# Two halves of a gathered tile's TensorE transposes, issued one step apart

## The chip, the cores and the metric

The kernel runs on one core of one Trainium2 chip. The metric is the device time of one execution in microseconds, of which the median of several runs is given. Lower is better.

The engines are named as in the profile: PE is TensorE (matmuls and transposes) and PEld its weight loads, DVE is VectorE, ACT is ScalarE, POOL is GpSimd, SP is SyncE.

## The reference

The kernel computes two residual blocks on 625 rows of 1024 floats. The first is a relational graph convolution on 20000 edges with two relations. The second, which holds the change, is a mixture of eight experts, each row going to its two best, beside two shared experts:

```python
gates = xf @ rW + rb
topk_vals, topk_idx = jax.lax.top_k(gates, TOP_K)          # 2 of 8
topk_probs = jax.nn.softmax(topk_vals, axis=-1)
...
h = _gelu(jnp.einsum('td,edh->eth', xf, W1) + b1[:, None, :])   # 1024 -> 256
y = jnp.einsum('eth,ehd->etd', h, W2) + b2[:, None, :]          # 256 -> 1024
moe = jnp.einsum('te,etd->td', w, y)
return (shared + moe).reshape(B, L, D)
```

The sizes are D = 1024 and 256 hidden columns; all is float32.

## The kernel before

**The experts on gathered rows.** Each row needs only two of the eight experts. The kernel sorts the (row, expert) pairs into `NJ` = 11 tiles of 128 slots. Seven of them (4 to 10) hold rows of one expert, three (0 to 2) hold two halves of 64 slots with an expert each, and one (3) four quarters of 32 slots. Which expert a part belongs to is known only at run time, so weights are addressed by a register (`w1a[:, bass.ds(e, 1)]`).

A tile's normalized rows are gathered from DRAM (`h2d`) by an indirect DMA that GpSimd issues. They lie there as 128 rows of 1024; the product needs them as eight blocks of 128 x 128 with the 1024 on the partitions. This turning is done in one of two ways, in `fetch`:

- Five tiles (4, 6, 7, 8, 9) are gathered by one DMA of full rows. TensorE turns them with eight transposes (line 1441), four into each of two PSUM banks of the tag `acc`, of which there are five. ScalarE copies the first bank to `xsT` (line 1447), VectorE the second (line 1445).
- Six tiles (5, 0, 1, 2, 10, 3; `by_quarters`) are gathered by four DMAs of a quarter of the columns each (line 1424). One VectorE transpose (line 1429) turns the whole tile.

**The loop.** The tiles go in the order 4, 5, 6, 0, 7, 1, 8, 2, 9, 10, 3. Step `s` of the loop issues three things, each for another tile: `fetch` of tile `s` (gather and turning), `expert_in` of tile `s - 1` and `expert_mid` of tile `s - 2`:

```python
for s in range(NJ + 2):
    if s < NJ:
        fetch(tiles[s])
    if 0 <= s - 1 < NJ:
        expert_in(tiles[s - 1])
    if 0 <= s - 2 < NJ:
        expert_mid(tiles[s - 2])
```

`expert_in` (line 1462) multiplies the turned tile by W1 in eight steps of 128 rows; the first four steps read the first half of `xsT`, the other four the second half. In the trace a step of a whole tile is two matmuls. VectorE copies the 256 columns of the result to `hj` (line 1466). `expert_mid` turns that by two TensorE transposes (line 1474), and ScalarE applies Gelu with the bias (line 1477). ScalarE also makes copies of W1 for the parts of tiles 0 to 3 behind the first (`copy_w1`, line 1456), four instructions in each of six steps.

**What sets the order.** Each engine works through its own queue in order, and in this stage the queues stand in the order in which the program issues. `tc.issue_after` puts an instruction behind another one on its engine: the VectorE transpose of a tile stands behind the last copy of line 1445 (`turned[-1]`), the copies of W1 behind the last ScalarE instruction kept in `acts`.

**Buffers.** The gathered rows `xs` have three buffers (pool `io`), so the gather of a tile waits until the tile three places earlier in the order has been turned: 0 for 4, 7 for 5, 1 for 6, 8 for 0, 2 for 7, 9 for 1, 10 for 8, 3 for 2. `xsT` and `hj` have two buffers each; products use PSUM banks of the tag `mm`, of which there are three.

After the stage the second products (line 1522) follow, then the scatter of their rows, the shared experts' output (line 1577) and the sum.

## Time and profile before

| | |
|---|---|
| median of 3 runs | 288.99 us (287.6 to 293.84) |
| the profiled execution, its own time | 290.18 us |
| its span, first to last instruction | 288.4 us |
| TensorE busy | 277.2 us (96%) |
| VectorE, ScalarE, GpSimd busy | 171.8, 100.2, 65.1 us |
| the chain that ended last, by engine | PE 82%, DVE 12%, issue 3%, ACT 1% |
| matmuls of line 1462 (expert_in) | 40.1 us and 14.7 us (copied W1) |
| transposes of line 1441, one | 0.275 us, 40 of them |
| copy of line 1445, one | 0.692 us, 5 of them |
| VectorE transpose of line 1429, one | 2.05 us, 6 of them |
| gather issue of line 1424, one | 0.949 us, 24 of them |

The profile page is one execution taken by the hardware profiler. Its times count from the first instruction. A line of the timeline gives the start and the length in us, the engine, the line of the kernel, the operation with what it writes and reads, the shape, the number of instructions merged into it (x8), and in brackets the idle time of the engine before it with what ended the wait. Matmuls are pipelined: their starts are recorded, their ends are modelled, so those of neighbours overlap. The stage of the change lies between 158 and 207 us.

### The profile page before, as it was taken

Reading aid. Unit: us, or ns where it says so; the run is one execution under the profiler, and the core shown is the slowest. Engines: PE = TensorE matmul, PEld = TensorE weight load, DVE = VectorE, ACT = ScalarE, POOL = GpSimd, SP = SyncE. Lnnn points to the kernel's source line nnn. Section 1 sums busy time; section 2 is a strip of 40 time slices with the busy share of each in tenths; the row PEclk is TensorE's granted clock in tenths of the full one; section 3 lists DMA queues with packets and bytes.
Section 4 is the critical chain, followed back from the end, with each engine's and each line's share of the span. In section 5 each row is a group of like instructions: output and inputs, shape, how many; then the busy total and the mean of one; then the engine's idle time right before and its main releaser. Section 6 shows DMA issues by size and latency. Waiting matters only on the chain.

```text
span 288.4 us, 4459 instructions
## 1 busy us (share of the span) xinstructions
PE 277.2 (96%) x1531; PEld 186.5 (65%) x1531; DVE 171.8 (60%) x433; ACT 100.2 (35%) x232; POOL 65.1 (23%) x128
## 2 busy tenths in 40 slices
PE   8999999999999999899999988999999999999991
PEld 6877777788888455677777877788543344444460
DVE  6899999999874898657800522446143111159820
ACT  3366328243642422453011414854397111000000
POOL 9910110000000124320151656541022222100000
PEclk9999999999999999999999999999999999999997
DMA  7999960000002999996999344321185545399441
GB/s 230 358 333 368 403 216 28 0 0 2 1 0 74 383 391 426 423 403 206 418 406 400 101 145 130 128 60 53 45 338 231 213 190 220 133 374 376 150 142 43
DMA packets 22107, 61.58 MB, mean 214 GB/s; under 512 B 2490, under 2 KB 8317, under 8 KB 21056
## 3 DMA queue, kind: packets, MB, share of 16 engines
q1 hardware_dynamic: 16106, 44.31, 41.3%
q0 software_dynamic: 5680, 16.58, 16.0%
q10 hardware_dynamic: 294, 0.35, 0.6%
q8 instruction: 14, 0.23, 0.3%
q14 instruction: 13, 0.11, 0.1%
HBM read 43.19 MB, written 18.82 MB: 215 GB/s over the span
## 4 chain that ended last, share of the span: by engine, by line
PE 82%; DVE 12%; issue 3%; ACT 1%; DVEq 0%; ACTq 0%
PE p_pr L944 18%; PE p_yj L1522 13%; PE p_o L1577 12%; PE p_h L1462 11%; PE p_sh L1209 11%; PE p_agg L961 5%; PE scrap L1024 2%; PE p_y L1007 2%; DVE xh L1011 2%; PE cnt L923 2%; DVE xsT L1429 1%; DVE st L776 1%; DVE h L749 1%; PE p_t L841 1%; PE p_gate L1155 1%
## 5 line engine op out<-in xcount | busy, mean ns | idle before, releaser
L944 PE MATMUL p_pr<-wg,nT 128*125 128x286 f32 x240 | 61.7, 408 | 0.5 <-ACT nT L847 0.3
L944 PEld LDWEIGHTS p_pr<-wg,nT 128*125 128x125 f32 x240 | 43.4, 187 | 12.7 <-ACT nT L847 1.4
L1462 PE MATMUL p_h<-w1a,xsT 128*128 (+2 forms) x176 | 40.1, 381 | 1.3 <-DVE xsT L1429 1.1
L1522 PE MATMUL p_yj<-w2a,hjT 128*128 (+2 forms) x88 | 38.6, 594 | 0.0
L1577 PE MATMUL p_o<-sw,shT 128*125 128x512 f32 (+1 forms) x88 | 36.1, 553 | 0.0
L1209 PE MATMUL p_sh<-h2T,sw 128*128 128x313 f32 (+1 forms) x128 | 35.3, 429 | 0.0
L1462 PEld LDWEIGHTS p_h<-w1a,xsT 128*128 128x128 f32 (+2 forms) x176 | 28.7, 168 | 8.1 <-issue 1.1
L1209 PEld LDWEIGHTS p_sh<-h2T,sw 128*128 128x128 f32 x128 | 23.6, 189 | 8.5 <-issue 0.2
L1522 PEld LDWEIGHTS p_yj<-w2a,hjT 128*128 128x128 f32 (+2 forms) x88 | 14.4, 168 | 22.4 <-issue 22.4
L1526 DVE COPY ys<-p_yj 128x512 f32<-128x512 f32 x15 | 10.4, 692 | 28.7 <-PE p_yj L1522 26.6
L1577 PEld LDWEIGHTS p_o<-sw,shT 128*125 128x125 f32 x88 | 16.4, 187 | 16.9 <-issue 16.2
L1424 POOL DMA_INDIRECT xs<-h2d,tok x24 | 22.8, 949 | 19.6 <-PE p_x L1441 7.3
L1018 POOL DMA_DIRECT2D x1d<-xh x10 | 5.9, 588 | 71.0 <-DVE flagf L726 62.0
L1466 DVE COPY hj<-p_h 128x256 f32<-128x256 f32 x11 | 4.6, 415 | 27.5 <-PE p_h L1462 12.5
L1530 POOL DMA_INDIRECT yt<-ys,row x11 | 10.7, 973 | 40.8 <-DVE ys L1526 40.8
L1007 PE MATMUL p_y<-wo_t,eT 128*125 128x512 f32 (+1 forms) x40 | 18.8, 592 | 0.0
L1477 ACT ACTIVATE hjT<-p_hT,vT 128x128 f32<-128x128 f32 (+2 forms) x34 | 8.8, 335 | 25.1 <-remote 11.0
L1553 DVE SCALAR_TENSOR_TENSOR x<-p_o,x 125x512 f32<-125x512 f32 (+1 forms) x11 | 6.9, 639 | 15.6 <-PE p_o L1579 15.6
L961 PE MATMUL p_agg<-P,CT 125*125 125x288 f32 x100 | 15.5, 305 | 0.0
L1462 PE MATMUL p_h<-w1m,xsT 128*64 128x256 f32 (+1 forms) x96 | 14.7, 381 | 0.0
L1522 PE MATMUL p_yj<-w2m,hjT 128*64 128x512 f32 (+1 forms) x48 | 14.1, 595 | 0.0
L899 DVE TENSOR_TENSOR ohs<-ohs,cols 125x1024 f16<-125x1024 f16 (+1 forms) x22 | 13.9, 633 | 0.0
(304 smaller groups left out, 412.0 us busy)
## 6 DMA issues: line engine op xcount, KB each, us to landing
w1a<-in_L_ffn_W_dram SPq DMA_DIRECT2D x8, 1024.0 KB
w2a<-in_L_ffn_W_dram SPq DMA_DIRECT2D x8, 1024.0 KB, 5.0
yt<-zero SPq DMA_DIRECT2D x2, 2560.0 KB
g<-yt SPq DMA_DIRECT2D x10, 512.0 KB, 7.3
sw<-in_L_ffn_sW_dram SPq DMA_DIRECT2D x4, 1024.0 KB, 6.2
x<-x1d SPq DMA_DIRECT2D x5, 500.0 KB
x1d<-xh POOLq DMA_DIRECT2D x5, 448.0 KB
h2d<-h POOLq DMA_DIRECT2D x5, 448.0 KB
```

Source lines behind the costliest of these rows:

```text
L899: last = nc.vector.tensor_tensor(os, os, both(VV_, 128)[1], op=ALU.mult)
L944: nc.tensor.matmul(p[:TP, :F], nT[:, k, m * TP : (m + 1) * TP], wg[:, k, r, :], start=(k == 0), stop=(k == KD - 1))
L961: nc.tensor.matmul(p[:TP, : F + 2], CT[:, m, at : at + TP], P[:, m, r, i], start=(m == 0 and i == 0), stop=(m == NT - 1 and i == 1))
L1007: nc.tensor.matmul(ps[s][:TP, :], eT[:n, k, :], wo_t[:n, k, at], start=(k == 0), stop=False)
L1209: nc.tensor.matmul(p[:, : z - a], sw1[:, i, k, t * 128 : (t + 1) * 128], h2T[:, k, a:z], start=(k == 0), stop=(k == KD - 1))
L1424: nc.gpsimd.indirect_dma_start(out=xs[:, a], out_offset=None, in_=h2d.rearrange("n (b f) -> (n b) f", b=4), in_offset=bass.IndirectOffsetO ...
L1462: nc.tensor.matmul(p[a:b, :H], xsT[j][:, k, a:b], w1m[j, a][:, 0, k, :] if a else w1a[:, bass.ds(e, 1), k, :], start=(k == 0), stop=(k == ...
L1477: done = nc.scalar.activation(hjT[:, j, t, a:b], p[:, t * 128 + a : t * 128 + b], AF.Gelu, bias=bT[:, bass.ds(e, 1), t])
L1522: made = nc.tensor.matmul(p[a:b], hjT[:, j, k, a:b], w2m[j, a, k][:, at] if a else w2a[:, bass.ds(e, 1), k, at], start=(k == 0), stop=(k = ...
L1526: nc.vector.tensor_copy(y[:, at], p)
L1530: sent.append(nc.gpsimd.indirect_dma_start(out=yt, out_offset=bass.IndirectOffsetOnAxis(ap=row[:, j : j + 1], axis=0), in_=y, in_offset=No ...
L1577: nc.tensor.matmul(p[:TP, :n], shT[:, i, k, own], sw2[:, i, k, at], start=(i == 0 and k == 0), stop=False)
```

## The change

The turning by TensorE is moved into a function `turn(j, g)` for one half. `fetch` issues only the first half. The second half is issued at the beginning of the next step, ahead of the next tile's `fetch` and so directly in front of the tile's own `expert_in`. The transposes, the copies, their engines and their buffers are the same; the gathered rows are read for the last time one step later.

```diff
         t_ = xt.tile([128, KD, 128], F32, tag="xsT", name=f"xsT_{j}")
-        for g in range(2):
-            p = ps_acc(f"p_x{g}_{j}")
-            for k in range(4):
-                nc.tensor.transpose(p[:, k * 128 : (k + 1) * 128], xs[:, 4 * g + k :: KD], ident)
-            o = t_[:, 4 * g : 4 * g + 4, :]
-            pv = p.rearrange("p (k n) -> p k n", k=4)
-            if g:
-                turned.append(nc.vector.tensor_copy(o, pv))
-            else:
-                acts.append(nc.scalar.copy(o, pv))
         xsT[j] = t_
+        half_row[j] = xs
+        turn(j, 0)
         copy_w1(j)
+
+    half_row = {}
+
+    def turn(j, g):
+        p = ps_acc(f"p_x{g}_{j}")
+        for k in range(4):
+            nc.tensor.transpose(p[:, k * 128 : (k + 1) * 128], half_row[j][:, 4 * g + k :: KD], ident)
+        o = xsT[j][:, 4 * g : 4 * g + 4, :]
+        pv = p.rearrange("p (k n) -> p k n", k=4)
+        if g:
+            turned.append(nc.vector.tensor_copy(o, pv))
+        else:
+            acts.append(nc.scalar.copy(o, pv))
...
     for s in range(NJ + 2):
+        if 0 < s <= NJ and tiles[s - 1] in half_row:
+            turn(tiles[s - 1], 1)
         if s < NJ:
             fetch(tiles[s])
```

## The prediction

> Names: T(j,0) and T(j,1) are the two halves of the transposes of tile j by TensorE, A(j) and V(j) their copies out of PSUM by ScalarE and VectorE, S(j) the VectorE transpose of a tile gathered by quarters, P(j) the eight products of expert_in, hj(j) the copy of its result, M(j) the two transposes of expert_mid. The tiles go 4, 5, 6, 0, 7, 1, 8, 2, 9, 10, 3; TensorE turns 4, 6, 7, 8 and 9.

> **What bounds the kernel.** First the page: the shares and the chain.

> ```profile
> span 288.4 us, 4459 instructions
> PE 277.2 (96%) x1531; PEld 186.5 (65%) x1531; DVE 171.8 (60%) x433; ACT 100.2 (35%) x232; POOL 65.1 (23%) x128
> PE 82%; DVE 12%; issue 3%; ACT 1%; DVEq 0%; ACTq 0%
> ```

> TensorE is the bound, so only its idle time can be won. The change touches the stage of the gathered tiles, 158 to 207 us. Next, the timeline of TensorE there:

> ```profile
> 158.09 1.06 PE L1441 MATMUL p_x<-ident,xs 128*128 128x128 f32 x8
> 159.37 3.72 PE L1462 MATMUL p_h<-w1a,xsT 128*128 x16 [0.23 <-ACT xsT L1447]
> 162.92 1.06 PE L1441 MATMUL p_x<-ident,xs 128*128 128x128 f32 x8
> 163.82 3.62 PE L1462 MATMUL p_h<-w1a,xsT 128*128 x16
> 167.28 0.38 PE L1474 MATMUL p_hT<-ident,hj 128*128 128x128 f32 x2
> 167.49 3.62 PE L1462 MATMUL p_h<-w1a,xsT 128*128 x16
> 171.96 0.44 PE L1474 MATMUL p_hT<-ident,hj 128*128 128x128 f32 x2 [0.85 <-issue]
> 172.24 1.05 PE L1441 MATMUL p_x<-ident,xs 128*128 128x128 f32 x8
> 174.04 0.40 PE L1462 MATMUL p_h<-w1a,xsT 128*64 x1 [0.75 <-DVE xsT L1429]
> ...
> 191.50 0.40 PE L1462 MATMUL p_h<-w1a,xsT 128*64 x1 [0.32 <-DVE xsT L1429]
> ```

> In order: T(4), P(4), T(6), P(5), M(4), P(6), M(5), T(7), P(0); the last line is P(2). The brackets are all the idle time of TensorE in the stage: 0.23 before P(4), 0.85 before M(5), 0.75 before P(0), 0.32 before P(2), together 2.15 us. Who made it wait is on VectorE:

> ```profile
> 163.12 0.42 DVE L1466 COPY hj<-p_h 128x256 f32<-128x256 f32 x1 [1.30 <-PE p_h L1462]
> 164.08 0.69 DVE L1445 COPY xsT<-p_x 128x512 f32<-128x512 f32 x1 [0.53 <-PE p_x L1441]
> 171.48 0.42 DVE L1466 COPY hj<-p_h 128x256 f32<-128x256 f32 x1 [6.72 <-PE p_h L1462]
> 171.82 2.07 DVE L1429 STREAM_TRANSPOSE xsT<-xs 128x1024 f32<-128x1024 f32 x1
> 173.81 0.39 DVE L1466 COPY hj<-p_h 128x256 f32<-128x256 f32 x1
> 174.11 0.68 DVE L1445 COPY xsT<-p_x 128x512 f32<-128x512 f32 x1
> 179.85 0.42 DVE L1466 COPY hj<-p_h 128x256 f32<-128x256 f32 x1 [5.06 <-remote]
> ```

> hj(4), V(6), hj(5), S(0), hj(6), V(7), hj(0). hj(4) starts 0.03 after P(4) ends (159.37 + 3.72). But P(5) ends at 167.44 (163.82 + 3.62) and hj(5) starts at 171.48: the signal of the finished product was **4.0 us late**, with VectorE idle. The same reading gives 2.1 us for hj(0), 2.7 for hj(1) and 1.4 for hj(2); none for hj(9) and hj(10). The Gelu of M(4), M(6), M(7) and M(8) is 4.5, 3.2, 3.0 and 1.7 us late in the same way. The stalls of 0.85 and 0.75 us are what is left of the 4.0 us. Last, GpSimd:

> ```profile
> 164.42 0.95 POOL L1434 DMA_INDIRECT xs<-h2d,tok  x1 [0.30 <-issue]
> ...
> 169.42 0.95 POOL L1424 DMA_INDIRECT xs<-h2d,tok  x1 [0.30 <-issue]
> 174.16 0.94 POOL L1434 DMA_INDIRECT xs<-h2d,tok  x1 [3.79 <-DVE xsT L1429]
> ```

> It issues gathers in trains with 0.30 us between them: 159.4 to 170.4, 174.2 to 180.1, 182.6 to 188.5, 191.6 to 196.3. All four late products end inside a train, and their signals come from 0.3 us before to 1.1 us after its end. A train is not enough: P(4) and T(6) signal on time inside the first, and what else it takes the rows do not say. Outside the trains the signals that an idle engine waits for (P(9), P(10), T(8)) are on time. This is a coincidence of few rows, and the forecast turns on it.

> **The change, part by part.** It adds and removes no instruction: 40 transposes, 5 copies on ScalarE, 5 on VectorE stay. TensorE's own work is the same to the instruction; no change in its sum. Tile 4 keeps its order, T(4,0), T(4,1), P(4): no change, the 0.23 stays. For tiles 6, 7, 8, 9 the second half moves past P and M of two other tiles on TensorE, past one hj on VectorE, and past nothing on ScalarE, whose half stays.

> *TensorE and the copy.* Eight transposes take 0.90 us of issue (162.92 to 163.82), a half 0.45. A product takes 3.46 (163.82 to 167.28), its first four steps 1.73. From the start of T(j,1): last transpose over at 0.60 (third start step 0.33 plus 0.27); V(j) starts 0.09 later (T(8) over at 182.65, V(8) at 182.74), takes 0.69, and TensorE takes up its result 0.15 later (S(0) over at 173.89, P(0) at 174.04): 1.53. The four steps that need only the first half last until 0.45 + 1.73 = 2.18. V(j), formerly covered by another tile's whole product, is now covered by these four steps with 0.65 us to spare: cost 0. Without the cover, each microsecond of lateness beyond 0.65 is a stall, four times.

> *VectorE.* New order: hj(5), V(6), S(0), hj(6). S(0) is behind V(6), which is behind a copy that could be late. With signals on time S(0) ends 1.38 + 2.05 = 3.43 after T(6,1) starts, and P(0) wants it at 0.45 + 3.46 + 0.22 + 0.45 = 4.58: covered by 1.1 us. Before P(10) no T stands: 0.45 + 3.46 + 0.22 = 4.13, covered by 0.7.

> *GpSimd's queue.* The three gather buffers go round, so the gathers of tiles 1, 2 and 10 wait for T(6,1), T(7,1) and T(8,1), some 4 us later than now, and the full-row gathers of 8 and 9 queue behind them. Tile 8: the quarters of tile 1 start 0.9 after T(6,1) does and take four times 1.25, so tile 8's gather starts near 5.9; T(8,0) comes three steps of 4.13, 12.4 us, after T(6,1). That leaves 6.5 us for a flight that now takes 4.2 (issued at 174.16, the traffic of the window's slices falls from 334 to 134 GB/s at 178.4). Cost 0, with 2.3 to spare. SyncE's next load, line 1501, waits for the last product of the stage and shifts with it; its data are wanted 40 us later.

> *The late signals.* Since GpSimd now waits for T(j,1), it is idle when P(5), P(0) and P(1) end and T(6,1), T(7,1), T(8,1) follow: no train runs at these three places. Then hj(5) and S(0) are early and the stalls of 0.85, 0.75 and 0.32 vanish: −1.92. At T(9,1) the train for tile 3 still runs, since it waits for S(2), not for a turn: late by 1.3 (M(8)'s 1.7 less the 0.45 of the half) gives a stall of 0.65; the longer train, to about 3 us past the end of P(2), gives about 2.2. No row shows which; I take 1.2, the nearer side of the middle. Sum: −1.92 + 1.2 = −0.7; bounds −1.92 and +0.3.

> The profiled execution took 290.18 us (span 288.4), so 289.5; the median of the runs is 288.99, 1.2 us under the profiled one, so the forecast on the runs' scale is **288.3 us**, own range 287.0 to 289.4.

> The rows show a signal 4.0 us after its product's end. [...]

> In the rows P(4) waits for A(4) and nothing behind it starts. [...]

> **Rivals.** *The signals stay late* and now meet the product itself. Place: the fifth step of P(6), P(7), P(8), P(9), waiting for V(j) behind hj on VectorE. The lateness of T(j,1) is that of M just before it less 0.45: 4.1, 2.8, 2.6, 1.3; less the cover of 0.65: 3.4, 2.1, 1.9, 0.6, together 8.0, against 1.92 saved: +6.1, **295.1 us**. If each is as long as the longest, 4 x 3.4 − 1.9 = +11.7, 300.7. For it: hj is late in four of four places of this kind, and TensorE now always waits at such a signal. Against: GpSimd's trains begin only after the signal. It decides once the lateness exceeds 0.65 + 1.92/4 = 1.1 us on average.

> *The gathers arrive late.* If the flights of tiles 8 and 9 take 4 us more than 4.2, T(8,0) and T(9,0) wait 1.7 each: +3.4 on my sum, 291.7. For it: the longer trains in front of them. Against: the cover of 2.3 us, and that other DMA traffic is over by 160.

> *It does nothing.* The stalls may belong to the profiled execution alone, whose time is above the median; then the order is another and the time 289.0.

> **How the numbers follow.** Forecast 0.46, late signals 0.40, late gathers 0.06, nothing 0.08. What a measurement of this kernel can tell from no change is about 2%, 5.8 us: 283.2 or 294.8. The forecast cannot reach the first, as all idle time of the stage is 2.15; I leave 0.03. Of the late signals, between 293 and 301, three quarters are above 294.8: 0.30, with 0.01 for other mishaps 0.31. The rest, 0.66, is within. The range goes from 286.8, all stalls gone with a little noise, to 297.5, which leaves out a quarter of the late signals.

> **What would show it.** Right: TensorE's first half of P(6) goes into its second without a gap; hj(5) starts within 0.1 us of the end of P(5); GpSimd idles from 165.4 to about 168; the stage ends near 206. Wrong: brackets of 2 to 3 us inside P(6) to P(9) with V(j), L1445 of the profile before, as releaser; or brackets before T(8,0) naming a gather.

## The result: 1.1% slower at first, and no difference on three later occasions

| | before | after |
|---|---|---|
| median of 6 runs each | 290.64 us (287.53 to 293.84) | 291.58 us (289.15 to 291.87) |
| ratio, with its 95% interval | | 1.0106 [1.0077, 1.0134] |
| the profiled execution, its own time | 290.18 us | 291.51 us |
| its span | 288.4 us | 289.6 us |
| T(4) to the eight products of line 1522 (after: 1529) | 49.77 us | 51.51 us |

The runs of before lie in two groups, 287.5 to 289.0 and 292.3 to 293.8; the ratio is formed with the lower group alone, while between the medians of all six the difference is 0.9 us, 0.3%, and three runs of before took longer than any of after. In the kernel after, the copy of T(j,1) is line 1452, that of T(j,0) 1454, the products 1467, hj 1471, expert_mid 1479, the second products 1529.

First the page of after, with the granted clock in 40 slices:

```profile
PE 278.5 (96%) x1531; PEld 185.9 (64%) x1531; DVE 171.9 (59%) x433; ACT 100.7 (35%) x232; POOL 64.9 (22%) x128
...
PEclk9999999999999999999999999997999999999999
```

TensorE is still the bound. A single slice, the 28th (195 to 203 us), has a lower clock. The timeline of TensorE, P(5) to P(6), then from T(9,1) to the start of P(10):

```profile
163.78 3.62 PE L1467 MATMUL p_h<-w1a,xsT 128*128 x16
...
167.46 0.61 PE L1448 MATMUL p_x<-ident,xs 128*128 128x128 f32 x4
167.90 3.62 PE L1467 MATMUL p_h<-w1a,xsT 128*128 x16
...
193.06 0.38 PE L1448 MATMUL p_x<-ident,xs 128*128 128x128 f32 x2
193.95 0.39 PE L1448 MATMUL p_x<-ident,xs 128*128 128x128 f32 x2 [0.51 <-issue]
194.17 0.38 PE L1467 MATMUL p_h<-w1a,xsT 128*128 x1
195.37 1.10 PE L1467 MATMUL p_h<-w1a,xsT 128*128 x3 [0.81 <-issue]
196.80 4.45 PE L1467 MATMUL p_h<-w1a,xsT 128*128 x12 [0.33 <-issue]
...
201.30 1.03 PE L1467 MATMUL p_h<-w1a,xsT 128*128 x4
```

The upper part is P(5), T(6,1) and P(6): P(6) runs through its fifth step without a gap, and the stalls of before at M(5), P(0) and P(2) are gone from the timeline. The lower part is T(9,1) in two pieces, P(9) in three, and P(10). The brackets shown add up to 1.65 us, and with one of 0.14 inside a merged row to 1.79 us. Their releaser is "issue": TensorE waited for nothing that the profile shows. The last twelve matmuls of P(9) take 4.45 us where sixteen take 3.62. VectorE beside it, hj(5), and then hj(2) and V(9); last ScalarE, the Gelu of M(8):

```profile
167.44 0.42 DVE L1471 COPY hj<-p_h 128x256 f32<-128x256 f32 x1 [3.47 <-PE p_h L1467]
...
197.00 0.42 DVE L1471 COPY hj<-p_h 128x256 f32<-128x256 f32 x1 [7.95 <-remote]
197.34 0.68 DVE L1452 COPY xsT<-p_x 128x512 f32<-128x512 f32 x1
...
197.04 0.63 ACT L1482 ACTIVATE hjT<-p_hT,vT 128x128 f32<-128x128 f32 x2 [4.72 <-remote]
```

hj(5) starts 0.04 us after P(5) ends (163.78 + 3.62), where it was 4.0 late before. hj(2) comes at 197.00, and P(2) had ended at 192.85: 4.1 us late, the only late copy of a product in the stage. The Gelu of M(8) comes at 197.04, and M(8) had ended at 193.22: 3.8 us late, with ScalarE idle. Both signals arrive when the gaps of TensorE end. In between TensorE goes on in steps of 0.7 us, with one to three starts in each (193.96, 194.68, 195.37, 196.09, 196.79). So lateness and gaps look like one event of some 4 us here; in the profile before, P(6) ran without a gap while hj(5) was late. GpSimd, the start of the second row of gathers, and the first and last gather of the last row:

```profile
168.34 0.95 POOL L1424 DMA_INDIRECT xs<-h2d,tok  x1 [2.56 <-PE p_x L1448]
...
185.41 0.94 POOL L1424 DMA_INDIRECT xs<-h2d,tok  x1 [2.58 <-PE p_x L1448]
...
194.16 0.95 POOL L1424 DMA_INDIRECT xs<-h2d,tok  x1 [0.30 <-issue]
```

The gathers of tiles 10 and 3 have become one row of eight, 185.41 to 195.1, and P(2) ends inside it. Last the clock, in windows (each engine's busy time, then the granted clock of TensorE, the DMA share and GB/s):

```profile
193.00:195.40 2.40, 1.08 (x8) 0.94 (x7) 0.00 (x0) 0.00 (x0) 1.81 (x2) 1.00 0.35 109
...
196.65:198.30 1.65, 1.50 (x4) 1.24 (x5) 1.30 (x3) 1.26 (x4) 0.00 (x0) 0.50 0.00 0
198.30:200.06 1.76, 1.76 (x6) 1.40 (x5) 1.69 (x1) 1.43 (x3) 0.00 (x0) 0.50 0.00 0
200.06:202.00 1.94, 1.94 (x12) 1.68 (x11) 0.49 (x2) 0.50 (x3) 0.00 (x0) 1.00 0.03 8
```

For 3.41 us the clock is one half, which loses 1.7 us. The account of the two first profiles: from T(4) to the end of P(2) after takes 34.35 us and before 37.09, 2.74 less (1.92 of it are the three stalls, 0.45 is T(9,1), which moved behind). From the end of P(2) to the start of P(10) it takes 8.45 and before 3.89: 0.45 is T(9,1), and **4.1 us are lost there**, of which 1.79 are gaps and 1.7 is the half clock. The remaining 0.37 and 0.6 fit the overlap that is lost at a gap (an estimate: a matmul of line 1467 lasts 0.38 us and the next otherwise starts after 0.22, so up to 0.16 for each of three and four gaps).

### The profile page after: what moved, and what is told of

The parts are those of the page before. It is cut to its first block, busy times and chain, and to the rows that moved or that the text cites. A ratio compares the mean times of both kernels' runs of the same rounds, so it can differ in the third digit from the quotient of the medians.

```text
span 289.6 us, 4458 instructions
## 1 busy us (share of the span) xinstructions
PE 278.5 (96%) x1531; PEld 185.9 (64%) x1531; DVE 171.9 (59%) x433; ACT 100.7 (35%) x232; POOL 64.9 (22%) x128
## 3 DMA queue, kind: packets, MB, share of 16 engines
q0 software_dynamic: 5680, 16.58, 15.8%
## 4 chain that ended last, share of the span: by engine, by line
PE 83%; DVE 8%; DMA 4%; issue 1%; SPq 1%; ACT 1%; ACTq 0%
PE p_pr L944 18%; PE p_h L1467 14%; PE p_yj L1529 13%; PE p_o L1584 12%; PE p_sh L1209 11%; PE p_agg L961 5%; DMA xh<-in_x_dram 4%; PE p_y L1007 2%; DVE xh L1011 2%; PE cnt L923 2%; PE p_x L1448 1%; DVE h L749 1%; DVE st L776 1%; PE p_hT L1479 1%; PE p_gate L1155 1%
## 5 line engine op out<-in xcount | busy, mean ns | idle before, releaser
L1467 PE MATMUL p_h<-w1a,xsT 128*128 (+2 forms) x176 | 42.3, 392 | 1.5 <-issue 1.1
L1467 PEld LDWEIGHTS p_h<-w1a,xsT 128*128 128x128 f32 (+2 forms) x176 | 29.9, 175 | 10.0 <-issue 2.1
L1424 POOL DMA_INDIRECT xs<-h2d,tok x24 | 22.8, 948 | 23.6 <-PE p_x L1448 15.0
```

What stands on the lines that cost most here:

```text
L1424: nc.gpsimd.indirect_dma_start(out=xs[:, a], out_offset=None, in_=h2d.rearrange("n (b f) -> (n b) f", b=4), in_offset=bass.IndirectOffsetO ...
L1467: nc.tensor.matmul(p[a:b, :H], xsT[j][:, k, a:b], w1m[j, a][:, 0, k, :] if a else w1a[:, bass.ds(e, 1), k, :], start=(k == 0), stop=(k == ...
```

## The experiments

**What makes the signals late, and does tile 9 decide?** Four kernels were run together on one chip. Theory T puts the late signals down to the rows of gathers, A to the register arithmetic that addresses W1.

*Halves apart for tiles 6, 7 and 8 only.*

```diff
         turn(j, 0)
+        if j == tiles[8]:
+            turn(j, 1)
...
-        if 0 < s <= NJ and tiles[s - 1] in half_row:
+        if 0 < s <= NJ and tiles[s - 1] in half_row and tiles[s - 1] != tiles[8]:
```

> The halves apart at tiles 6, 7 and 8 only; tile 9 is turned whole, as before. Theory T (gather trains: TensorE's signals and its own queue go slow while a product ends deep inside an unbroken row of gather issues, and the late T(8,1) joins the gathers of tiles 10 and 3 into one row of eight): the three stalls at tiles 6, 7, 8 stay away (TensorE's P(2) ends about 34.5 to 35 us after T(4) starts, against 37.1 before), the row of eight gathers is still there (185 to 195 us), the signal of P(2) is still about 4 us late and TensorE's queue still starves for 1 to 2 us around P(9); V(9) is no longer behind it, so part of the 4 us lost there comes back: 0 to +1.5 us against the kernel before, ratio 1.000 to 1.005. Rival R (taking tile 9's halves apart is itself the loss, by the wait at the fifth step of P(9)): no gap at P(9), the time 1.9 us under the kernel before, ratio 0.993.

*Halves apart for tile 9 only* (the same edit with the two comparisons exchanged).

> The halves apart at tile 9 only; tiles 6, 7 and 8 are turned whole. Theory T: the gathers of tile 10 follow T(8) early as before, the row of four for tile 3 (starting after the VectorE transpose of tile 2) is not joined to them, so P(2)'s signal is 1.3 to 2 us late as before and the fifth step of P(9) waits 0.6 to 1 us; no half-speed clock; the stalls of 0.85 and 0.75 stay. Against the kernel before +0.3 to +1 us, ratio 1.001 to 1.004. Rival R (the loss is the split at tile 9): the whole 4.1 us lost between P(2) and P(10) is there, without the 2.4 won earlier: +4 us, ratio 1.014.

*W1 at fixed addresses.*

```diff
-                                 w1m[j, a][:, 0, k, :] if a else w1a[:, bass.ds(e, 1), k, :],
+                                 w1m[j, a][:, 0, k, :] if a else w1a[:, j % NE, k, :],
```

> The changed kernel, but the products of expert_in read W1 at fixed places instead of places given by a register (so the first part of each tile gets a fixed expert's weights). Theory T1 (the train alone slows TensorE's signals): P(2)'s signal is still about 4 us late, TensorE idles 1.5 to 2 us at P(9); ratio to the kernel before 1.005 to 1.013. Rival A (it is the address arithmetic in TensorE's queue that goes slow during a train and holds the queue and its signals up): no late signal, no gap in P(9), no half-speed clock: about 4 us less than the changed kernel, ratio 0.990 to 0.996.

*One gather of full rows in place of four of quarters.*

```diff
-            for a in range(4):
-                nc.gpsimd.indirect_dma_start(
-                    out=xs[:, a], out_offset=None, in_=h2d.rearrange("n (b f) -> (n b) f", b=4),
-                    in_offset=bass.IndirectOffsetOnAxis(ap=tok4[:, a, j : j + 1], axis=0))
+            nc.gpsimd.indirect_dma_start(
+                out=xs.rearrange("p a f -> p (a f)"), out_offset=None, in_=h2d,
+                in_offset=bass.IndirectOffsetOnAxis(ap=tok[:, j : j + 1], axis=0))
```

> The changed kernel, but a tile turned by VectorE is gathered by one DMA of full rows instead of four of a quarter (so those six tiles hold their rows in another layout, and their products are of permuted data). Theory T: no row of gathers is longer than 2.5 us, no signal of TensorE is late, TensorE idles less than 0.6 us in the stage, no half-speed clock: 4 us less than the changed kernel, ratio to the kernel before 0.990 to 0.995. Rival R (the wait at the fifth step, whatever GpSimd does): gap and time as in the changed kernel, ratio 1.008 to 1.013.

| kernel | median, us | ratio to before | idle of TensorE in the stage |
|---|---|---|---|
| 6, 7, 8 apart | 287.44 | 0.9996 [0.9974, 1.0018] | 0.23 us |
| 9 apart | 287.26 | 0.9985 [0.9963, 1.0007] | 0.23 us |
| fixed W1 | 287.85 | 1.0019 [0.9997, 1.0041] | 0.23 us |
| one gather | 287.34 | 1.0000 [0.9980, 1.0021] | 0.23 us |
| before (35 runs) | 287.66 | 1 | |

None of the four has a late signal. The first still has the row of eight gathers (184.75 to 194.4) and the second a row of ten (160.9 to 173.1; the longest in the first profile of before has nine, 159.4 to 170.4), and hj starts on time in both. So neither T nor A can be judged: what they explain isn't there. Whether the kernel before still had late signals here was not known, so both kernels were profiled again.

**The two kernels once more, without a change.** This was done three times, on three chips; which chip the first profiles came from isn't recorded.

> The kernel before once more, with a profile of its own. The four variants run so far on another chip show no late signal of TensorE at all and no idle time in the stage but 0.2 us, the rows of gathers being as long as ever. Theory C (the late signals come and go with the chip and the time, the kernel only decides what they hit): on this chip the stalls of 0.85, 0.75 and 0.32 us are either all gone, with hj(5) within 0.1 us of the end of P(5), or there with hj(5) several us late. Theory T (the late signals belong to the kernel's rows of gathers): they are there as in the first profile, 1.9 us of stalls. Ratio to the runs of the kernel before beside it 1.000.

> The changed kernel once more. Theory C: where the signals are on time there is no stall to save and no cost either, the copy being covered by four steps: TensorE idles 0.2 us in the stage and the ratio to the kernel before is 0.997 to 1.003. Theory T (the joined row of eight gathers costs 4 us at tile 9, always): signal of P(2) 4 us late, 1.8 us of gaps around P(9), ratio 1.008 to 1.013.

> The kernel before, profiled on this call's chip as the neighbour of the other three. No late signal and 0.2 us idle in the stage if this chip is like the last two; late signals of 1 to 4 us and 1 to 2 us idle if it is like the first.

> The changed kernel on the same chip. If the kernel before shows no late signals here: stage and time equal within 0.3%, ratio 0.997 to 1.003. If it shows them: they hit this kernel at tile 9, where the gathers of tiles 10 and 3 form one row of eight, with 2 to 4 us lost there and 1.9 us won at tiles 6 to 8, ratio 1.003 to 1.013.

> The kernel before, once more, in the hope of the conditions of the first profiles. Where copies of finished products start more than 0.5 us after the product's end (hj(5) 4.0 us in the first profile): brackets of 0.3 to 0.9 us before M(5), P(0) or P(2), some 2 us in all. Where they are on time, as in the two later profiles: TensorE idles 0.23 us in the stage and the time is 287 to 288.

> The changed kernel, once more, beside the kernel before. With signals on time, within 0.3% of the kernel before and a stage without gaps (0.23 us). With late signals: theory G (they come inside rows of GpSimd's gathers): lateness at P(2) alone, inside the row of eight gathers of tiles 10 and 3, with gaps of about 1.8 us around T(9,1) and half clock after them, about 1% slower than the runs of the kernel before; rival O (they come at any place): lateness at other products too, gaps at the fifth step of P(6), P(7) or P(8).

| pair | before | after | after less before |
|---|---|---|---|
| second | 287.25, 0.9977 [0.9952, 1.0001] | 286.91, 0.9977 [0.9954, 1.0000] | −0.34 us |
| third | 287.64, 1.0009 [0.9986, 1.0033] | 287.38, 1.0023 [1.0003, 1.0044] | −0.26 us |
| fourth | 287.17, 1.0012 [0.9991, 1.0034] | 287.21, 1.0002 [0.9980, 1.0024] | +0.04 us |

The ratios are to more runs of the kernel before in the same job. The kernels are equal to 0.4 us, and in none of the six profiles is a signal late. The timeline of TensorE of the kernel before, second profile, P(5), M(4), P(6), M(5):

```profile
164.40 3.62 PE L1462 MATMUL p_h<-w1a,xsT 128*128 x16
167.86 0.38 PE L1474 MATMUL p_hT<-ident,hj 128*128 128x128 f32 x2
168.08 3.62 PE L1462 MATMUL p_h<-w1a,xsT 128*128 x16
171.53 0.38 PE L1474 MATMUL p_hT<-ident,hj 128*128 128x128 f32 x2
```

And its VectorE at hj(5):

```profile
168.06 0.42 DVE L1466 COPY hj<-p_h 128x256 f32<-128x256 f32 x1 [2.71 <-PE p_h L1462]
```

P(5) ends at 168.02 and hj(5) starts 0.04 later, inside an unbroken row of gathers; M(5) follows P(6) with no bracket. The 0.85, 0.75 and 0.32 us are not there to be won. The kernel after, second profile, at the place where 4.1 us had gone:

```profile
192.59 0.61 PE L1448 MATMUL p_x<-ident,xs 128*128 128x128 f32 x4
193.03 3.62 PE L1467 MATMUL p_h<-w1a,xsT 128*128 x16
196.49 0.38 PE L1479 MATMUL p_hT<-ident,hj 128*128 128x128 f32 x2
196.70 3.62 PE L1467 MATMUL p_h<-w1a,xsT 128*128 x16
```

T(9,1), P(9), M(2), P(10) without a gap, though the row of eight gathers is there as well. From T(4) to the eight products after the stage, the three pairs: before 47.43 to 47.44 us, after 47.38 to 47.39. The first profiles had 49.77 and 51.51. So the first occasion added 2.3 us to before and 4.1 us to after, and the change itself 0.0.

*Tiles 6, 7 and 8 apart, again.*

> The halves apart for tiles 6, 7 and 8 only; tile 9's second half straight behind its first, as in the kernel before. With signals on time, as the first time: 0.9996 of the kernel before within its interval. With late signals as in the first profile of the changed kernel: P(2)'s copy late as there, but no half of a turn waits behind it, so the gaps shrink to 0.3 us (as before P(2) in the profile before) and the clock stays at 1.00; 3.5 us under the changed kernel of the same runs.

287.75 us, 1.0028 [0.9999, 1.0057], idle 0.23 us. Without late signals it says nothing on tile 9.

**How much cover has the late half?** The order of the product's steps is turned round, so that the late half is wanted first.

```diff
-        for k in range(KD):
+        for n, k in enumerate((*range(4, KD), *range(4))):
...
-                                 start=(k == 0), stop=(k == KD - 1))
+                                 start=(n == 0), stop=(n == KD - 1))
```

> The changed kernel, with the eight steps of every product in the order 4 to 7, 0 to 3, so that the half turned last is read first and its copy has no cover. If the cover of 1.73 us was what hid the copy: each of P(6), P(7), P(8), P(9) waits 1.53 - 0.45 = 1.1 us at its first step, P(4) 0.5 us longer than now, about 4.8 us in all; ratio to the kernel before about 1.016. Rival (the copy is hidden by something else, or TensorE's pipeline works it off): no wait over 0.3 us, ratio within 0.3% of the changed kernel's.

288.49 us, 1.0021 [0.9998, 1.0044]: 1.6 us more than the kernel after beside it, not the 4.8 that were expected. The reason is in the timeline of TensorE:

```profile
157.70 1.57 PE L1448 MATMUL p_x<-ident,xs 128*128 128x128 f32 x12
159.54 7.17 PE L1467 MATMUL p_h<-w1a,xsT 128*128 x32 [0.27 <-DVE xsT L1452]
...
166.77 0.61 PE L1448 MATMUL p_x<-ident,xs 128*128 128x128 f32 x4
168.29 1.17 PE L1448 MATMUL p_x<-ident,xs 128*128 128x128 f32 x8 [0.92 <-DMA xs<-h2d,tok]
```

T(6,0) now stands with T(4) (x12), P(4) and P(5) back to back (x32), and both halves of T(7) (x8) behind T(6,1) (x4), ahead of P(6). So the queue does not stand in the order of the program here, as it does in this stage of the kernels before and after: other work stands where the waits were expected. That it was put there because of them is inferred, not shown. What is left is 0.27 us and a wait of 0.92 for a gather that is now wanted earlier. The cover wasn't measured by this; it is read from the second profile of after instead: T(6,1) at 166.99, V(6) at 167.69 for 0.69 us, P(6) at 167.43, so its fifth step is due at 169.16. V(6) is over at 168.38 and, with the 0.15 us from the end of S(0) to P(0) in the first profile of before (173.89 to 174.04), can be taken up at 168.53 (an estimate from these rows): **0.63 us to spare** where 0.65 was predicted.

*The copy of tile 9 done six times*, to make a gap at one place.

```diff
-            turned.append(nc.vector.tensor_copy(o, pv))
+            turned.append([nc.vector.tensor_copy(o, pv) for _ in range(6 if j == tiles[8] else 1)][-1])
```

> The changed kernel, but VectorE's copy of the second half of tile 9 is done six times over, so that TensorE stands idle at one place, at the fifth product step of tile 9; TensorE's queue differs from the changed kernel's in one place, the two transposes of tile 2's expert_mid, which now stand between the fourth and the fifth step of that product (0.27 us of cover). Copies follow each other by 0.60 us, so V(9) ends 3.0 us later, at 196.98 in the times of the last profile of the changed kernel (it started at 193.29); the fifth step is due at 193.03 + 1.73 + 0.27 = 195.03, TensorE takes a result up 0.15 later: a bracket of 2.1 us there, releaser L1452. Theory C (a gap of about 2 us also lowers the granted clock for the microseconds that follow, as in the first profile of the changed kernel, where 1.79 us of gaps were followed by 3.4 us at half clock): +2.1 and half of 3.4, +3.8 us, 290.7, and a window of about 3.4 us with a granted clock of 0.50 behind the gap. Rival I (the gap alone): +2.1 us, 289.0, and a granted clock of 1.00 throughout; then the half clock of the first profile had another cause.

286.83 us, 0.9994 [0.9966, 1.0023], and neither theory: there is no gap. TensorE in its timeline:

```profile
193.44 1.89 PE L1467 MATMUL p_h<-w1a,xsT 128*128 x8
...
195.38 3.60 PE L1529 MATMUL p_yj<-w2a,hjT 128*128 x8
198.82 5.34 PE L1467 MATMUL p_h<-w1a,xsT 128*128 x24
```

Between the fourth and the fifth step of P(9) stand M(2) and eight products of the next stage (p_yj), 3.6 us of work that is due later anyway, so the order differs here too, at the place of the expected wait. The granted clock is 1.00 throughout, and whether a gap of 2 us would lower it stays untested.

**Does other DMA traffic make the signals late?** Theory D. Six stores of SyncE run during the stage, in both kernels:

```diff
+    junk = dram.tile([6 * 128, NS * HK * N], F32, name="junk")
+    for i in range(6):
+        nc.sync.dma_start(junk[i * 128 : (i + 1) * 128], shT.rearrange("p a b n -> p (a b n)"))
```

> The kernel before with added work that nothing reads: once the shared experts' hidden rows are done (about 158 us), SyncE starts six DMAs of 1.28 MB each from SBUF to DRAM, so that other traffic runs beside the gathers for most of the stage. Theory D (late signals of TensorE come from pressure on the DMA side, which another job or another moment can bring): hj(5), hj(0), hj(1) or hj(2) start more than 1 us after the end of their products, as in the first profile, and TensorE stalls 1 us or more before M(5), P(0) or P(2). Rival: the signals stay within 0.1 us; then only the gathers' flights get longer, with stalls that name a gather.

> The changed kernel with the same added traffic. Theory D: signals late as well, and now they fall on the fifth step of P(6) to P(9): TensorE stalls more than in the kernel before with the traffic, by 1 to 4 us. Rival: signals on time; the gathers of tiles 1, 2, 10, which start some 3 to 4 us later than in the kernel before, and those of 8, 9 and 3 behind them, have less room for a longer flight, so waits that name a gather come at T(8,0), T(9,0) or at the VectorE transpose of tile 3, where the kernel before has none or shorter ones: 0 to 3 us more than the kernel before with the traffic.

Before with traffic 295.76 us, 1.0285 [1.0208, 1.0363]; after with traffic 295.13, 1.0293 [1.0238, 1.0348]. At over 400 GB/s no product's signal is late; in this form and on this chip D falls. What costs the time in the profiles is one wait of TensorE for a gather in each, T(7) before and T(7,0) after (the added lines move its transposes to line 1452):

```profile
177.49 1.97 PE L1441 MATMUL p_x<-ident,xs 128*128 128x128 f32 x8 [6.13 <-DMA xs<-h2d,tok]
```

```profile
175.79 1.12 PE L1452 MATMUL p_x<-ident,xs 128*128 128x128 f32 x4 [4.84 <-DMA xs<-h2d,tok]
```

Both also show what follows a long gap. Windows of after with traffic, from the end of the gap, then two of before with traffic:

```profile
175.79:178.00 2.21, 2.21 (x10) 1.48 (x12) 0.00 (x0) 0.59 (x1) 0.00 (x0) 0.50 1.02 421
178.00:179.00 1.00, 1.00 (x6) 0.47 (x4) 0.00 (x0) 0.00 (x0) 0.00 (x0) 0.50 1.00 409
179.00:180.00 1.00, 1.00 (x12) 0.66 (x10) 0.00 (x0) 0.00 (x0) 0.00 (x0) 0.89 1.04 428
...
171.40:177.50 6.10, 0.01 (x1) 0.01 (x1) 2.32 (x2) 0.62 (x2) 0.94 (x1) 0.91 1.02 424
...
183.00:183.60 0.60, 0.60 (x8) 0.33 (x6) 0.00 (x0) 0.00 (x0) 0.29 (x2) 0.77 0.98 401
```

In after the clock is one half until 179.22 (0.22 of the third window at 0.50 give its mean of 0.89): 3.4 us, as long as in the first profile of after. The price is 4.84 + 1.7 = 6.5 us; the profiled execution, 293.00, lies 5.9 over the median of before beside it, 287.08. In the kernel before the half clock begins 1.1 us before the gap is over (the mean of 0.91 over 6.10 us) and ends at 183.28 (0.77 over 0.60): the trace's record of the clock has 176.45 to 183.28, 6.83 us, twice 3.41. 5.8 us of it follow the gap: 6.13 + 2.9 = 9.0, and 296.36 lies 9.3 over it.

## Why the prediction was wrong

*Bound, order and cover were right.* TensorE is the bound; V(j) and S(j) are covered; GpSimd idles before each row (165.8 to 168.34, said was 165.4 to 168); hj(5) starts 0.04 us after P(5). In the first profile of after the stalls at M(5), P(0) and P(2) vanished, as forecast. No product ever waits at its fifth step for V(j), so the rival of the signals that meet the product itself (295.1 us) did not occur.

*The term −1.92 came true in the first profile of after and is nothing in the later ones.* The step took three stalls of one profile for time that the kernel always loses. In three later profiles of before TensorE idles 0.23 us in the stage, all of it before P(4), so there is nothing to win: the term is 0, and the rival "It does nothing", given 0.08, describes three pairs out of four. The prediction had the warning in hand: the profiled execution, 290.18, was 1.2 us over the median, and P(4) and T(6) signalled on time inside a train.

*The term +1.2 at tile 9 failed, in size and in kind, and it made the first result.* From T(4) to the eight products after the stage the first profile of after takes 1.74 us more than that of before, where the sum had −0.7. The place was right, T(9,1) beside the long row. The term stood between 0.65 and 2.2 (its own premise, 3 us past the end of P(2), less the 0.45 and the cover of 0.65, gives 1.9). The row ended 2.3 us past P(2), the signal came 4.1 past it, and 4.1 us were lost there; in the three later profiles of after the term is 0. The gaps, 1.79, are inside the bounds, but they do not lie at the fifth step: T(9,1) and the first steps of P(9) pause, waiting for nothing that the profile shows, and V(9) has no part in it. The half clock after them, 1.7 us, was in no term of the sum.

*So the measured +1.1% has a place but no shown cause.* In the profile the time is lost between P(2) and P(10), together with late signals, at the row of eight gathers that the change makes. That this row is enough is refuted by all three later profiles of after and by the first kernel with tiles 6, 7 and 8 apart, which have it and lose nothing. Register addresses weren't tested where signals were late, and added traffic did not bring lateness about. Whether the recording of the trace has a part in it wasn't tested. Whether the change makes the loss likelier where signals are late, or the profile of after met a worse moment than that of before, stays open: no later run met the first condition.

## What to carry to other kernels

A stall in one profile is a saving only if a second profile of the same kernel shows it; an engine that starts 4 us after its releaser has finished, in a row where its neighbours start at 0.04, is a reason to profile again before a change is costed. A gap of TensorE can cost more than its length: with added traffic, after 4.84 and 6.13 us of waiting, the clock was one half for 3.4 and 5.8 us more, while after 0.85 and 0.75 us in the first profile of before it stayed at 1.00, and the run with the late half first, with its wait of 0.92 us, has a mean of 0.997. An edit that is meant to make a gap has to be read in the queue's order first: twice here other work stood in the place of the gap. Moving work of a saturated engine by one step, with the copies covered before and after, moved no time that shows (−0.34 to +0.04 us in the three later pairs).

## What the runs showed of the hardware

**Completions.** The late signals come with another trait of the first occasion. Between 160 and 200 us the trace holds 125 (before) and 112 (after) increments of the semaphores on which the gathers land, and 366 to 375 in the twelve later profiles of kernels with the same gathers and no added traffic; up to 150 us all of these have 1694 to 1727 on all semaphores. The packets are the same, 5680 in that queue. In the first profiles a gather shows 1 to 16 increments, mostly 3 to 5, later 16 with few exceptions. The trait alone does not make a signal late: in the first profile of after the increments are few from 160 us on, 83 until 190 us against 278 in the second, while every copy of a product starts on time until P(2). Whether increments were lost, merged or only not recorded, the traces don't say. That is a coincidence in time, and its cause was not found.
